# The first two of sixteen batches handled each alone in the sorting and gathering stages of a graph network

## The chip, the cores and the metric

The kernel runs on one core of a Trainium2 chip. A core has a matrix engine (PE, with its weight loads shown apart as PEld), a vector engine (DVE), a scalar engine (ACT), a general engine (POOL) and a queue engine that here only starts transfers (SP). The metric is device time in microseconds (us), the median over runs. "Faster" and "slower" are meant against the kernel before, run on the same chip.

## The reference

Sixteen batches of 1024 nodes with 64 features each and a 0/1 adjacency matrix of 1024 x 1024 (about 4 neighbours a node) go through four residual layers, each `x = x + layer(max(layernorm(x), 0), adj)`:

- layer 0: product with the adjacency plus self-loops, scaled on both sides by the root of the degree, times a 64 x 64 matrix, relu;
- layer 1: three such hops one after the other, all four stages together times a matrix, plus a bias;
- layer 2: for each node a weighted sum of three quantiles (0.25, 0.5, 0.75) of each feature over its neighbours and itself, then a two-layer perceptron. A node with more than ten neighbours first loses some of them, and the loss holds for both ends of an edge;
- layer 3: a plain adjacency product of a 64 x 64 transform, plus a bias.

```python
sv = jnp.sort(jnp.where(valid[..., None], x[:, None, :, :], big), axis=2)
pos = jnp.clip(tau * (m - 1.0), 0.0)          # m: number of valid neighbours
q = gather(floor(pos)) * (1 - frac) + gather(ceil(pos)) * frac
agg = sum(weight * q)                          # weights 0.25, 0.5, 0.25
```

## The kernel before

Layer 2 needs, for each node, the rows of its neighbours next to each other, so that a sorting network can compare them feature by feature. The kernel takes the batches two by two: eight pairs. For each pair there are two halves of work, both written in `fast` (L2044).

`first(pair)`:

- *graph0*, *graph1* (`fast_graph`, L1273), one for each batch: eight tiles of 128 adjacency rows come from memory by SP into one of four row buffers; PE transposes them, ACT writes them as fp8 into `at`, ACT and DVE count, and DVE finds the positions of the first eight neighbours (`found`).
- *lists* (`by_degree`, L1303, and `dilated`, L1396): the 2 x 1024 nodes are ordered by degree into 16 blocks (`S`), each with 64 nodes (`HP`) of one batch on the lower 64 partitions and 64 of the other on the upper. Nodes of block 0 may have more than eight neighbours: POOL fetches their full adjacency rows by an indirect transfer into `high` (L1407), and DVE reads them in `past` (L1414). The stage ends with the index lists `idx` and the quantile weights.
- *layers0*, *layers1* (`fast_to_table`, L1794): layers 0 and 1 of one batch, that is four adjacency products (`prod`), each with an ACT pass `u` behind it; then the normalised `h` is written by ACT's DMA queue into `table`, a tensor in memory with the rows of both batches.
- *rare* (`packed`, L1515): the few nodes with more than nine valid entries get their further indices packed.

`second(pair)`:

- *gather16*, *gather8*, *gather5* (`fast_quantiles`, L1601): POOL issues one indirect transfer (`gather`, L1532) for each block and neighbour number, which puts 128 rows of `table` into `slots`. `CAPS` says how many a block needs, `GROUPS` which blocks are sorted together: block 0 alone in a network of 16, blocks 1 to 6 in networks of 8, blocks 7 to 15 in networks of 5. Block 0 has nine transfers of its own, one of packed rare indices (`got`, L1537, which PE spreads with the matmuls `rare`) and one for the node itself; the others have `CAPS` plus itself. That is 86 for a pair. The last pair cuts the third group into a 5 and a 4.
- *sort16*, *sort8*, *sort5* (`compared`, L1558): DVE runs the compare-exchange networks and sums by weight into `agg`, which is split into three 16-bit parts.
- *unsort* (`unsorted`, L1711): back to node order. For each block DVE writes a 0/1 matrix `back`, and PE multiplies the three parts with it: 16 blocks x 3 parts x 2 batches x 2 halves = 192 matmuls with 64 contracted rows each.
- *out0*, *out1* (`fast_to_output`, L1870): perceptron, layer 3, result to memory.

The program calls `first(0)`, and then for each pair `first(pair + 1)` and `second(pair)`. This is not the order of execution: every operation is noted by `Plan.note` (L361), and `Plan.order` (L412) arranges all of them by a list scheduler, with a modelled duration and landing time (`cost`, L506) and a due time for each stage and pair (`WANTED`, L149, 23 stages x 8 pairs). `Plan.issue` then emits them in that order from L495, so nearly every instruction in the trace stands at L495 and is told apart by its operands. Each engine's queue is thus one fixed order; POOL's holds the `high` gathers and the row gathers of all pairs one behind the other. In `cost`, an indirect transfer takes 1.38 and lands after

```python
return 1.38, 1.7 if out.shape[-1] < N else 3.5      # L513-514; out of N or more: the high rows
```

in the scheduler's own units; these are not measured times.

Tables exist more than once and are used in turn (`self.tables[pair % len(self.tables)]`), and so are the buffers of each phase.

Of the kernel before, what the change touches and what calls it, by code (L numbers as in the profile page):

```python
# [23 lines left out]
P = 128  # L24
# [3 lines left out]
F = 64  # L28
# [12 lines left out]
CAPS = (15, 7, 6, 6, 5, 5, 5, 4, 4, 4, 3, 3, 3, 2, 2, 1)  # L41
GROUPS = ((0, 1, 16), (1, 7, 8), (7, 16, 5))
PAY = E + 3

NETS = (
# [49 lines left out]
WEIGHED = (  # L95
# [4 lines left out]
ADDED = (  # L100
# [4 lines left out]
LAST_GROUPS = (*GROUPS[:-1], (7, 12, 5), (12, 16, 4))  # L105
LAST_NETS = (
    *NETS[:-1],
# [21 lines left out]
    *WEIGHED[:-1],  # L129
# [4 lines left out]
    *ADDED[:-1],  # L134
    ((5, 0, 2, 2), (5, 0, 1, 1)),
    ((3, 0, 1, 2), (1, 1, 2, 3), (4, 0, 1, 1)),
)
FULL = 1
# [11 lines left out]
    "cells": (-238, 424, 470, 815, 927, 816, 1455, 1240),  # L150
    "const": (-127, -97, -54, -87, -26, 53, 92, 130),
    "gather16": (-320, 656, 868, 854, 1050, 1295, 1563, 1378),
    "gather4": (932, 827, 907, 1006, 1324, 1439, 1758, 1922),
    "gather5": (718, 624, 460, 714, 1049, 1015, 1225, 1795),
    "gather8": (-187, 861, 1244, 1124, 1559, 1596, 1708, 1672),
    "graph0": (121, 435, 480, 407, 973, 766, 1340, 1470),
    "graph1": (-272, 331, 531, 808, 1245, 1113, 1408, 2213),
    "layers0": (70, -98, 97, 77, 308, 585, 1093, 1356),
    "layers1": (263, 464, 588, 915, 832, 1050, 1312, 2006),
    "lists": (124, 563, 698, 686, 965, 1121, 1451, 1437),  # L160
    "out0": (-133, 489, 557, 659, 1058, 1166, 1508, 2220),
    "out1": (-24, 70, 154, 231, 695, 804, 1077, 1509),
    "rare": (340, 337, 385, 505, 923, 954, 1478, 1312),
    "sort16": (-64, 647, 651, 894, 1226, 1187, 1475, 1758),
    "sort4": (252, 1204, 1304, 1422, 1709, 1881, 2198, 1916),
    "sort5": (248, 1092, 1063, 1277, 1658, 1352, 2202, 1597),
    "sort8": (-310, -3, -266, 45, 246, 232, 788, 950),
    "strike": (267, 762, 802, 915, 1177, 1361, 1733, 2291),
    "unsort16": (348, 373, 375, 447, 889, 957, 1237, 1085),
    "unsort4": (226, 294, 346, 425, 709, 861, 1140, 920),  # L170
    "unsort5": (395, 460, 451, 701, 1158, 1004, 1359, 1044),
    "unsort8": (428, 583, 525, 959, 933, 1459, 1499, 1074),
# [132 lines left out]
class Carved:  # L305
# [6 lines left out]
    def tile(self, shape, dtype, name, tag=None):  # L312
# [21 lines left out]
        return self.made[key]  # L334

# [170 lines left out]
def cost(engine, op, out, ins, kw):  # L506
# [6 lines left out]
    if op == "indirect_dma_start":  # L513
        return 1.38, 1.7 if out.shape[-1] < N else 3.5
# [40 lines left out]
class Kernel:  # L555
    phase = ""

    def __init__(self, tc, ins, out):
        self.tc, self.nc, self.ins, self.out = tc, tc.nc, ins, out
        self.B = ins["x"].shape[0]  # L560


    def constants(self, pool, work):
# [18 lines left out]
        pair_of = self.counted(pool, work, "pair_rows", [self.B // 2], [[-FIRST, self.B // 2]], step=1)  # L582
        late = work.tile([P, self.B // 2], F32, name="late_rows")
# [35 lines left out]
        for name in ("L1_gnn_b", "L2_gnn_b2", "L3_gnn_bias"):  # L619
            t = pool.tile([P, F], F32, name=f"bias_{name}")  # L620
            nc.gpsimd.dma_start(
                out=t, in_=ins[name].rearrange("(o f) -> o f", o=1).to_broadcast([P, F])
            )
            self.bias[name] = t
# [15 lines left out]
        self.over = pool.tile([P, self.B // 2], F32, name="over")  # L640
# [18 lines left out]
    def sorted_constants(self, pool, work):  # L659
        nc = self.nc  # L660
        pairs = self.B // 2
# [42 lines left out]
        self.table_at = pool.tile([P, 1], F32, name="table_at")  # L704
        nc.gpsimd.tensor_scalar(self.table_at, late, float(N + 1), None, ALU.mult)
        pair = self.counted(work, work, "pair_of", [pairs], [[2, pairs]])
        nc.gpsimd.tensor_tensor(pair, pair, late.to_broadcast([P, pairs]), ALU.add)
        self.row_at = pool.tile([P, pairs], F32, name="row_at")
        nc.gpsimd.tensor_scalar(self.row_at, pair, float(N), None, ALU.mult)
        self.cell_at = pool.tile([P, pairs], F32, name="cell_at")  # L710
        nc.gpsimd.tensor_scalar(self.cell_at, pair, float(N * N), None, ALU.mult)
# [8 lines left out]
        self.caps = pool.tile([P, S], F32, name="caps")  # L720
        near = (NEAR, *CAPS[1:])
        for c in sorted(set(near)):
            a = near.index(c)
            nc.vector.memset(self.caps[:, a : a + near.count(c)], float(c))
# [3 lines left out]
        self.spare = pool.tile([P, 1], F32, name="spare")  # L728
        nc.gpsimd.tensor_scalar(self.spare, place, float(FIRST), None, ALU.is_ge)
# [7 lines left out]
        for n, (k, w) in enumerate(SHARED):  # L737
            nc.gpsimd.tensor_scalar(held, place, float(w), None, ALU.is_lt)
            nc.gpsimd.tensor_tensor(self.caps[:, 0:1], self.caps[:, 0:1], held, ALU.add)
# [48 lines left out]
        self.rows = [pool.tile([P, N + E], F32, name=f"row{n}") for n in range(ROWS)]  # L788
        self.high = pool.tile([P, N + E], F32, name="high")
        for r in [*self.rows, self.high]:  # L790
            nc.vector.memset(r[:, N : N + E], 1.0)
        self.slots = [
            pool.tile([P, hi - lo, n, F], F32, name=f"slots{n}") for lo, hi, n in GROUPS
# [421 lines left out]
    def redo(self):  # L1215

        nc, tc = self.nc, self.tc
        with ExitStack() as ctx:
            pool = self.pool(ctx, "redo", 1)
            self.off_diag = pool.tile([P, P], BF16, name="off_diag")  # L1220
            self.keys = pool.tile([P, N], F16, name="keys")
            self.pools(ctx, "redo", False)
            batch = pool.tile([1, self.B // 2, 2], F32, name="batch_flags")
            for i in range(2):
                flags = self.any_node(
                    pool,
                    self.ps_tr,
                    f"batches{i}",
                    self.over,
                    self.halves[:, i : i + 1],  # L1230
                    [(self.struck[:, i, n : n + 1], self.pair_rows) for n in range(2)],
                )
                nc.vector.tensor_copy(batch[:, :, i], flags)
            batch = batch.rearrange("o a b -> o (a b)")
# [68 lines left out]
    def by_degree(self, pair, zeros, founds):  # L1303
# [4 lines left out]
        pay = self.pay[pair % len(self.pay)]  # L1308
        hot = p.tile([P, 2, T, C], BF16, name="hot")
        for i in range(2):  # L1310
# [13 lines left out]
            b = 2 * pair + i  # L1324
            nc.scalar.copy(pay[:, mine, E + 2], self.mask[:, b * T : (b + 1) * T])
        w = T * C
        tb_ps = self.ps_tr.tile([w, 2, P], F32, name="tb", tag="tr")
        tb = p.tile([w, 2, P], BF16, name="tb_sb")
        for i in range(2):
# [3 lines left out]
        ps = self.ps_tr.tile([P, 2, w], F32, name="ranks", tag="tr")  # L1333
        for i in range(2):
# [3 lines left out]
        mine = p.tile([P, 2 * w], F32, name="mine")  # L1338
# [6 lines left out]
        rank = p.tile([P, 2 * T], I32, name="rank")  # L1345
        nc.vector.tensor_reduce(rank, mine.rearrange("p (s c) -> p s c", c=C), AX.X, ALU.add)
        place = p.tile([P, 2 * T], I32, name="place")
        nc.vector.tensor_scalar(place, rank, HP - 1, None, ALU.bitwise_and)
        tile_of = p.tile([P, 2 * T], I32, name="tile_of")
        nc.vector.tensor_scalar(tile_of, rank, 6, None, ALU.arith_shift_right)  # L1350
        tile_hot = p.tile([P, 2 * T, S], F16, name="tile_hot")
        nc.vector.tensor_tensor(
            tile_hot,
            self.sixteen.unsqueeze(1).to_broadcast([P, 2 * T, S]),
            tile_of.unsqueeze(2).to_broadcast([P, 2 * T, S]),
            ALU.is_equal,
        )
        there = self.p_lists.tile([P, 2 * T, HP], F16, name="there", bufs=1)
        nc.vector.tensor_tensor(
            there,  # L1360
            self.numbers[:, 0:HP].unsqueeze(1).to_broadcast([P, 2 * T, HP]),
            place.unsqueeze(2).to_broadcast([P, 2 * T, HP]),
# [3 lines left out]
        for a in range(0, 2 * T, HT):  # L1366
            shape = [P, HT, S, PAY]
# [6 lines left out]
        ps = self.ps_tr.tile([P, S, PAY], F32, name="sorted", tag="tr")  # L1374
        for t in range(T):
            for i in range(2):
                nc.tensor.matmul(
                    ps[i * HP : (i + 1) * HP].rearrange("p s c -> p (s c)"),
# [6 lines left out]
        near = self.p_lists.tile([P, S + 1, E], F32, name="near")  # L1385
        nc.scalar.copy(near[:, 0, :], ps[:, 0, 0:E])
        nc.scalar.copy(near[:, 2 : S + 1, :], ps[:, 1:S, 0:E])
        who = self.p_lists.tile([P, S + 1], F32, name="who")
        nc.scalar.copy(who[:, 0:1], ps[:, 0, E + 1 : E + 2])
        nc.scalar.copy(who[:, 1 : S + 1], ps[:, :, E + 1])  # L1390
        allowed = self.p_lists.tile([P, 1], F32, name="allowed")
        nc.scalar.copy(allowed, ps[:, 0, E + 2 : E + 3])
        nc.scalar.copy(self.degrees[pair], ps[:, :, E])
        return near, who, allowed

    def dilated(self, pair, near, who, allowed):  # L1396
# [4 lines left out]
        counts, gone = self.counts[pair], self.gone[pair]  # L1401
# [3 lines left out]
            at_row, who[:, 0:1], float(N - 1), self.row_at[:, pair : pair + 1], ALU.min, ALU.add  # L1405
# [15 lines left out]
        both = p.tile([P, 2, S + 1, E], F32, name="both")  # L1421
        own, good = both[:, 0], both[:, 1]
        nc.vector.tensor_tensor(
            own, near, who.unsqueeze(2).to_broadcast([P, S + 1, E]), ALU.is_equal
# [25 lines left out]
        for n in range(2):  # L1450
# [14 lines left out]
            base, who[:, 0:1], self.cell_at[:, pair : pair + 1], None, ALU.add  # L1465
# [6 lines left out]
        for i in range(2):  # L1472
            nc.sync.dma_start(
                out=self.cells[pair * FIRST : (pair + 1) * FIRST, i, :],
# [7 lines left out]
        idx = self.p_lists.tile([P, S + 1, E], U32, name="idx")  # L1482
        nc.vector.tensor_scalar(idx, near, float(N), self.table_at, ALU.min, ALU.add)
        near_h = self.p_lists.tile([P, 2 * E], F16, name="near_h")
        nc.vector.tensor_scalar(near_h, near16, float(N), None, ALU.min)
        self_idx = self.p_lists.tile([P, S], U32, name="self_idx")
        nc.vector.tensor_scalar(
            self_idx, who[:, 1 : S + 1], float(N - 1), self.table_at, ALU.min, ALU.add
# [222 lines left out]
    def unsorted(self, sums, hs, who):  # L1711
# [6 lines left out]
        for i in range(2):  # L1718
            self.turned(ps[i], hs[i])
# [486 lines left out]
```

## Time and profile before

| | |
|---|---|
| median of 9 runs | 1952.91 us (1937.44 to 1965.82) |
| the profiled execution's own time | 1961.34 us |
| its span in the profile | 1959.5 us |
| its mean granted PE clock | 0.737 of full speed |
| instructions | 23508 |
| row gathers by lists (`slots<-table,idx`) | 544, busy 556.2 us, 1022 ns each |
| row gathers of the nodes themselves | 124, busy 118.7 us, 957 ns each |
| matmuls `prod<-back,agg_high` | 256, busy 67.0 us |
| DVE `back` | 128, busy 61.4 us |
| first row gathers of the eight pairs at | 140, 365, 591, 813, 1033, 1249, 1462, 1680 us |

How to read it: the profile gives, for each engine, its busy time and the groups of like instructions with their number, busy time and mean duration; the idle time before a group is put down to what ended it, which is another instruction, a DMA, "issue" (nothing that the profile shows) or "remote" (another core or a queue that the profile does not know). A window cuts a stretch out of the span and gives the busy time and the number of instructions of each engine in it. PE, DVE, ACT and POOL run side by side, so busy shares don't sum to one.

### The profile page before, as it was taken

The page shows a single profiled execution, that of the slowest core. Times are in us where ns is not written, and L with a number is a line of the kernel's source. Part 1 is how long each engine was busy: PE and PEld are TensorE (multiplying, and loading weights), DVE is VectorE, ACT ScalarE, POOL GpSimd, SP SyncE. Part 2 cuts the span into 40 slices and gives each one's busy share as a digit, 9 for nine tenths or more (in the row PEclk, how much of TensorE's full clock was granted, in tenths as well). Part 3 has the DMA queues.
Part 4 walks back from the last instruction along what each step waited for, and adds up shares of the span by engine and source line. Part 5 has one row for each costly group of instructions (what it writes and reads, how often), then busy time and mean ns, then how long its engine had stood idle before and what let it go on. Part 6 is the DMA issues. An engine that isn't in the chain of part 4 may idle for free.

```text
span 1959.5 us, 23508 instructions
## 1 busy us (share of the span) xinstructions
PE 1161.4 (59%) x8497; PEld 626.9 (32%) x8497; DVE 925.9 (47%) x2408; ACT 733.2 (37%) x2024; POOL 757.6 (39%) x846
## 2 busy tenths in 40 slices
PE   3981638745697728756396729838386637411535
PEld 2551324422353315423152305514152324100312
DVE  6730617911296507824295506933296225700391
ACT  5860428601382406604282407704282222100202
POOL 8117160446207270354406470463417171574000
PEclk9985668856698758857597858867587668655767
DMA  7231222201222113212231212311221010110000
GB/s 211 89 89 27 70 65 104 60 18 43 62 87 54 53 32 99 69 25 79 54 98 31 67 36 82 100 34 44 65 84 30 8 40 6 32 27 16 11 1 13
DMA packets 93885, 108.49 MB, mean 55 GB/s; under 512 B 65120, under 2 KB 65232, under 8 KB 93760
## 3 DMA queue, kind: packets, MB, share of 16 engines
q1 hardware_dynamic: 18944, 67.12, 10.2%
q0 software_dynamic: 23744, 27.13, 7.4%
q10 hardware_dynamic: 51072, 12.66, 3.0%
q8 instruction: 68, 1.11, 0.2%
q14 instruction: 57, 0.47, 0.1%
HBM read 98.45 MB, written 8.39 MB: 55 GB/s over the span
## 4 chain that ended last, share of the span: by engine, by line
PE 37%; another core or an unknown queue 23%; DVE 15%; issue 12%; ACT 9%; DMA 1%; POOL 1%; ACTq 0%; DVEq 0%; POOLq 0%
PE prod L495 25%; PE node L495 8%; ACT u L495 5%; DVE slots L495 4%; DVE side L495 3%; ACT junk L495 2%; DVE found L495 2%; PE tr L495 1%; ACT at L495 1%; PE hidden L495 1%; DVE back L495 1%; DVE st L495 1%; PE rare L495 1%; DVE rest L495 1%
## 5 line engine op out<-in xcount | busy, mean ns | idle before, releaser
L495 POOL DMA_INDIRECT slots<-table,idx x544 | 556.2, 1022 | 245.8 <-issue 161.5
L495 PE MATMUL prod<-at,low 128*64 128x512 fp8e4 x1280 | 238.1, 405 | 57.1 <-issue 52.1
L495 PE MATMUL prod<-at,rest 128*64 128x512 fp8e4 x1280 | 240.3, 411 | 53.1 <-issue 43.5
L495 PE MATMUL prod<-at,u 128*64 128x512 fp8e4 x1280 | 237.9, 414 | 33.9 <-issue 19.9
L495 ACT ACTIVATE u<-node,d 128x64 f32<-128x64 f32 x640 | 141.3, 341 | 217.6 <-remote 162.6
L495 DVE TENSOR_SCALAR back<-numbers,who 128x1024 bf16<-128x1024 f16 x128 | 61.4, 492 | 321.6 <-remote 281.0
L495 POOL DMA_INDIRECT got<-table,rare x8 | 11.6, 1445 | 485.4 <-DMA table<-h 197.9
L495 PE MATMUL prod<-back,agg_high 64*64 64x512 bf16 x256 | 67.0, 494 | 201.3 <-issue 102.6
L495 ACT COPY rest<-prod 128x512 f32<-128x512 f32 x80 | 47.2, 590 | 302.9 <-remote 135.8
L495 DVE FIND_INDEX8 found<-ones,row 128x8 uint32<-128x1032 f32 x128 | 156.9, 1228 | 0.0
L495 PE MATMUL tr<-ident_bf,row 128*128 128x128 bf16 x1024 | 91.5, 244 | 101.1 <-ACT at L495 75.2
L495 ACT ACTIVATE junk<-row,unit 128x1024 fp8e4<-128x1024 f32 x122 | 143.5, 1177 | 16.2 <-DMA row<-in_adj_dram 14.3
L495 ACT ACTIVATE u<-x,off,by 128x64 f32<-128x64 f32 x384 | 134.6, 445 | 37.1 <-DVE off L495 23.3
L495 ACT ACTIVATE at<-tr 128x1024 fp8e4<-128x1024 bf16 x128 | 130.9, 1045 | 26.1 <-remote 17.2
L495 DVE TENSOR_TENSOR rest<-u 128x512 f32<-128x512 f32 x80 | 55.0, 688 | 165.7 <-ACT u L495 147.6
L495 POOL DMA_INDIRECT slots<-table,self_idx x124 | 118.7, 957 | 37.8 <-issue 37.2
L495 PEld LDWEIGHTS <-low 128*64 128x64 bf16 x1280 | 82.3, 115 | 147.2 <-issue 79.9
L495 PEld LDWEIGHTS <-rest 128*64 128x64 bf16 x1280 | 82.9, 116 | 140.5 <-issue 72.9
L495 PE MATMUL node<-wbd,ft_sb 128*128 128x128 f32 x512 | 101.3, 311 | 34.0 <-issue 28.3
L495 PEld LDWEIGHTS <-u 128*64 128x64 bf16 x1280 | 78.5, 116 | 119.4 <-issue 59.0
L495 PEld LDWEIGHTS <-row 128*128 128x128 bf16 x1024 | 74.6, 111 | 127.4 <-issue 107.7
L495 PEld LDWEIGHTS <-agg_high 64*64 64x64 bf16 x512 | 25.4, 125 | 251.8 <-issue 180.2
(254 smaller groups left out, 2144.3 us busy)
## 6 DMA issues: line engine op xcount, KB each, us to landing
row<-in_adj_dram SPq DMA_DIRECT2D x128, 512.0 KB
slots<-table,idx POOLq DMA_INDIRECT x544
x<-in_x_dram ACTq DMA_DIRECT2D x32, 128.0 KB
table<-h ACTq DMA_DIRECT2D x32, 128.0 KB
out_dram<-u ACTq DMA_DIRECT2D x32, 128.0 KB
slots<-table,self_idx POOLq DMA_INDIRECT x124
cells<-cell SPq DMA_DIRECT2D x16, 0.2 KB
side<-in_L_gnn_W_dram POOLq DMA_DIRECT2D x2, 64.0 KB
```

What stands on the lines that cost most here:

```text
L495: f(*[real(x) for x in s.args], **{k: real(x) for k, x in s.kw.items()})
```

## The change

The list of pairs becomes a list of nine sets: batch 0 alone, batch 1 alone, and then the seven pairs of the other fourteen. A set of one batch has 8 blocks of 128 nodes instead of 16 blocks of 2 x 64. Its `CAPS`, `GROUPS` and networks are cut to that: blocks 1 to 3 in networks of 8, blocks 4 to 7 in networks of 5, and 9 + 1 + 1 + 28 + 7 = 46 gathers a set. Its unsort has 8 blocks x 3 parts x 2 halves = 48 matmuls with 128 contracted rows. Tables of a single set hold one batch.

The assumed landing of the high rows in the scheduler's model goes from 3.5 to 8.0, and `WANTED` gets new due times for 23 stages x 9 sets. Over the whole program the order written out holds 92 row gathers where the first pair had 86, and one more `high` gather; 7786 planned PE instructions instead of 7869; and 2341 of DVE instead of 2209.

The four row buffers become slices of one tile, the slots of the last pair's extra group lie in those rows, and three bias rows are kept in a work area and read again in the part that handles batches which don't fit (`redo`).

```diff
-CAPS = (15, 7, 6, 6, 5, 5, 5, 4, 4, 4, 3, 3, 3, 2, 2, 1)
-GROUPS = ((0, 1, 16), (1, 7, 8), (7, 16, 5))
+CAPS = {
+    1: (15, 6, 5, 5, 4, 3, 3, 2),
+    2: (15, 7, 6, 6, 5, 5, 5, 4, 4, 4, 3, 3, 3, 2, 2, 1),
+}
+GROUPS = {1: ((0, 1, 16), (1, 4, 8), (4, 8, 5)), 2: ((0, 1, 16), (1, 7, 8), (7, 16, 5))}
...
+FEWER = ({1: 1}, {6: 3, 3: 1, 1: 0}, {9: 4, 8: 4, 6: 3, 3: 1})
+
+def fewer(net, tiles):
+    out = []
+    for n, wires, how, *kept in net:
+        if tiles[n]:
+            kept = [{k: (tiles.get(m, 0), a, z) for k, (m, a, z) in x.items()} for x in kept]
+            out.append((tiles[n], wires, how, *kept))
+    return tuple(out)
+
+NETS = {1: tuple(fewer(n, t) for n, t in zip(PAIR_NETS, FEWER)), 2: PAIR_NETS}
...
-    "gather16": (-320, 656, 868, 854, 1050, 1295, 1563, 1378),
+    "gather16": (-251, 395, 865, 1154, 1076, 1352, 1519, 1989, 1587),
...
     if op == "indirect_dma_start":
-        return 1.38, 1.7 if out.shape[-1] < N else 3.5
+        return 1.38, 1.7 if out.shape[-1] < N else 8.0
...
+        b = range(self.B)
+        self.sets = [b[0:1], b[1:2], *(b[n : n + 2] for n in range(2, self.B, 2))]
...
-        for s in range(S):
+        for s in range(deep):
...
-                for i in range(2):
+                for i in range(many):
                     for h in range(2):
-                        mine = slice(i * HP, (i + 1) * HP)
+                        mine = slice(i * wide, (i + 1) * wide)
...
-        for pair in pairs:
-            if pair + 1 < len(pairs):
-                first(pair + 1)
+        for g in range(len(self.sets)):
+            if g + 1 < len(self.sets):
+                first(g + 1)
             else:
                 self.strike()
-            second(pair)
+            second(g)
```

Here `many` is the number of batches in the set, `wide` is 128 divided by it, and `deep` the number of blocks, 8 or 16.

## The prediction

> **What bounds the kernel now.** I read the page first, then the waits, then windows and timelines around the first gathers. The sum is made against the profiled execution: 1961.34 us, of which the span is 1959.5. That is 8.4 us (0.4%) above the median of 1952.91 us, so what comes out as a difference is laid on the median. About 0.5% is what a measurement of this kernel can tell from no change; the nine runs alone lie between 1937.44 and 1965.82.
>
> On the page no engine is full, PE the most, and the chain that ended last goes through four engines and through "issue" and "unknown" time. The costliest group is the row gathers of POOL.
>
> ```profile
> PE 1161.4 (59%) x8497; PEld 626.9 (32%) x8497; DVE 925.9 (47%) x2408; ACT 733.2 (37%) x2024; POOL 757.6 (39%) x846
> ...
> PE 37%; another core or an unknown queue 23%; DVE 15%; issue 12%; ACT 9%; DMA 1%; POOL 1%; ACTq 0%; DVEq 0%; POOLq 0%
> ...
> L495 POOL DMA_INDIRECT slots<-table,idx x544 | 556.2, 1022 | 245.8 <-issue 161.5
> ```
>
> So I looked in the waits for what the unknown time is (waited for: us in total, times, longest):
>
> ```profile
> DVE back L495 <- remote: 281.0, 24, 56.2
> PE prod L495 <- issue: 234.8, 115, 27.9
> ACT u L495 <- remote: 204.2, 8, 41.7
> ...
> POOL got L495 <- DMA table<-h: 197.9, 3, 88.5
> ```
>
> "Remote" and "issue" name no instruction of this core. Their place shows in the table of windows (window, length, then busy us and count of PE, PEld, DVE, ACT, POOL, then the granted clock, DMA share, GB/s):
>
> ```profile
> 140.00:158.00 18.00, 12.83 (x83) 8.14 (x84) 4.09 (x7) 9.88 (x19) 13.73 (x14) 0.69 0.31 83
> 158.00:204.00 46.00, 0.48 (x5) 0.32 (x4) 1.57 (x5) 1.75 (x8) 34.77 (x37) 0.54 0.14 26
> 204.00:250.00 46.00, 35.53 (x272) 21.84 (x273) 32.62 (x79) 28.93 (x84) 0.65 (x1) 0.75 0.21 71
> 300.00:365.00 65.00, 56.33 (x500) 31.17 (x500) 56.01 (x159) 58.12 (x155) 0.00 (x0) 0.90 0.35 114
> 365.00:424.00 59.00, 30.97 (x240) 15.91 (x240) 29.64 (x60) 15.01 (x52) 46.17 (x42) 0.72 0.13 23
> ```
>
> From 140 us on POOL issues gathers back to back. PE goes on for 18 us, then executes 5 matmuls in 46 us, and is back as soon as the stream ends. Two rows of ACT's timeline in that stretch (start, length, instruction, idle before) show that this is not a wait for data of the program: nothing runs for 34.30 us, and the matmuls that `u` reads had ended by 156.8.
>
> ```profile
> 156.88 0.19 ACT L495 ACTIVATION_READ_ACCUMULATOR junk<-row,unit 128x1 f32 x1
> 191.37 1.75 ACT L495 ACTIVATE u<-node,d 128x64 f32<-128x64 f32 x8 [34.30 <-remote]
> ```
>
> The second kind is the stream of 365 to 424 us: 42 gathers at 1.40 us, and PE still at 240 matmuls, half of the dense rate of 500 in 65 us. **So gather time and PE time mostly add up** instead of lying beside each other; POOL is 39% busy and still on the path. A pair takes some 219 us: 86 gathers at 1.25 us, 107 us, and about as much dense PE work.
>
> A page of the Trainium skill speaks against this reading: "SBUF — State Buffer", section "Who interferes with whom", says that PE and ACT never wait for another engine at these ports, and DMAs contend with no engine. By it PE would work through the stream; the windows of this case say otherwise, and they decide.
>
> **The change part by part.**
>
> *a. The first table comes earlier.* POOL's first gather waits for the table:
>
> ```profile
> 140.25 1.46 POOL L495 DMA_INDIRECT got<-table,rare  x1 [63.90 <-DMA table<-h]
> 142.01 0.95 POOL L495 DMA_INDIRECT slots<-table,idx  x1 [0.30 <-issue]
> 143.26 0.94 POOL L495 DMA_INDIRECT slots<-table,idx  x1 [0.30 <-issue]
> ```
>
> It now needs both batches; afterwards batch 0 alone. ACT's timeline shows batch 0's chain, one `u` from each product to the next:
>
> ```profile
> 56.25 0.72 ACT L495 ACTIVATE u<-node,d 128x64 f32<-128x64 f32 x3
> ...
> 71.47 1.72 ACT L495 ACTIVATE u<-node,d 128x64 f32<-128x64 f32 x8
> ...
> 83.43 1.71 ACT L495 ACTIVATE u<-node,d 128x64 f32<-128x64 f32 x8
> ...
> 96.22 1.74 ACT L495 ACTIVATE u<-node,d 128x64 f32<-128x64 f32 x8 [1.03 <-PE node L495]
> ```
>
> Steps of 15.2, 12.0 and 12.8 us. The last, to 116.7, took 20.5 because batch 1's products lie between; alone I take the mean of the two before, 12.4. Then 7.8 to the last `h` (116.7 to 124.5), 2.7 from the last table DMA to the gather (137.5 to 140.2). From 56.2: 56.2 + 15.2 + 12.0 + 12.8 + 12.4 + 7.8 + 2.7 = 119, against 140: 21 us earlier. Bounds: 127 if batch 1 still lies between, 101 if PE order alone decides (508 planned PE instructions stand ahead of this gather instead of 693, and 137.5 x 508/693 = 101).
>
> *b. Batch 0's gathers.* 8 blocks of 128 need 9+1+1+28+7 = 46 gathers: 46 x 1.25 = 57.5 us, so to 177. This stream is like that of 140 to 204: PE runs for some 12 to 18 us and stops to about 182 (5 us after the end, as at 204). If PE kept going, batch 1 would not be held at all.
>
> *c. Batch 1.* About one product of it is done by 131. After 182 its chain is 15.2 + 12.0 + 12.8 + 12.4 + 7.8 + 2.7 = 63: gathers from 245. PE needs less: 950 - 508 = 442 planned instructions between the two tables, at 0.14 us (65 us / 500 matmuls x 8497 records / 7869 planned) 62, of which 10 are over. Before, POOL's second stream stood from 251 to 296.
>
> *d. Batch 1's gathers and the third table.* 46 more. If at 1.40 us with PE half alive (the row of 365) they end at 309, with some 220 of the 575 instructions that are still ahead of the third table (1525 - 950) done; the other 355 take 50: gather at **361**. If PE stops in this stream too, it ends at 303, PE is back at 308, and a chain of 63 to 72 and 9 us of queue give 371 to 388. If neither stream stops PE, about 345. Before: 365. I take 361, as the table of batches 2 and 3 is ready only because PE already has their two graphs to do meanwhile, as in the stream of 365: -4.
>
> *e. Less PE work.* The two single sets unsort with 2 x 8 x 3 x 2 = 96 matmuls of 128 rows instead of 192 of 64; 96 x 0.262 (67.0 us / 256, the `agg_high` row) = 25 us of PE. The written order agrees: after the table of batches 2 and 3, 5544 instead of 5696 planned PE instructions up to the last table, 152 x 0.14 = **-21**; behind the last table 717 instead of 677, **+6**. They count in full only in dense stretches, as 300 to 365; nothing if PE waits there anyway.
>
> *f. What is added.* Networks: a pair's take 15, 22 and 16 us; a single set's 15, 11 and 7 by their tiles, so 2 x 33 - 53 = +13; lists, 16 us a pair, are done once more on half the width: 0 to +16. Together +13 to +29 of DVE. Cover: the stretch of 158 to 250 in which DVE is busy 34 of 92 us. I cost it at nothing; without the cover, up to +29. Six more gathers, 92 for 86, and one `high` gather are in the streams of b and d.
>
> *g. The later arrival (3.5 to 8.0).* It moves only the order. `past`, which reads the high rows, starts 60 to 80 us behind its gather in pairs 1 to 6; only in pair 0 does DVE wait for it, 1.0 us. Worth 0 to -1.
>
> *h. New due times* re-order every set. No row shows their worth. The gathers of the pairs start at 365, 591, 813, 1033, 1249, 1462, 1680: periods of 226, 222, 220, 216, 213, 218. If all six were as the best, -37; as the worst, +41. I take 0, the middle, and keep these ends for the range.
>
> **Sum:** -4 - 21 + 6 = -19 in 1961: 1942, and on the median **1934 us**.
>
> **The rivals.**
>
> *Same.* The third table is late by what the stopped PE costs: 371 to 388 instead of 361, so +6 to +23 in the place of -4; with -15 of e: -9 to +8, **1944 to 1961**. For it: the row of 158 to 204 is what a first gather stream looks like here, and there would be two; a start 21 us earlier is only a stop 21 us earlier. Against it: more PE work is ready at 245 than at 158.
>
> *Slower.* Batch 0's stream freezes batch 1's chain, and everything of batches 2 and 3 queues behind batch 1 on PE. The gathers for batches 2 and 3 start at 380 to 388 (+15 to +23), and the DVE work of f, which then meets the lists and networks of the next pairs in the dense stretch (DVE 56 of 65 us in 300 to 365), has no cover: +13 to +29. With -15 of e, +13 to +37, in the middle +25: **1966 to 1990**, middle 1978. It decides if fewer than some 100 matmuls are executed between 135 and 175 us and the third table's gather is later than 380. Against it: the page's DVE is 47% busy, and DVE stands still in such streams (`back` 281 us for "remote"), so there is room.
>
> *Larger gain.* PE works through batch 0's stream, because 46 gathers are fewer than 57: third table at 345, -20 - 15 = -35, and due times on the good side: **1895 to 1918**.
>
> *The change doesn't do what it says:* the earlier table isn't used, because POOL's fixed order holds something of batch 1 ahead of batch 0's gathers (before, the `high` gather of pair 1 held the second half of the stream to 251). The order written out has batch 0's 46 in one piece, so I give it no time of its own; it would fall under "same".
>
> **Chances.** Forecast (1918 to 1943) 0.40; larger gain 0.08; same 0.17; slower 0.35. Faster by over 0.5% is thus 0.48, within 0.5% 0.17, slower 0.35. The range has to reach into the slower case: 1900 to 1980 leaves out some 0.05 below (h at its best) and 0.13 above. The forecast's own range is 1918 to 1943.
>
> **What would show it.** a: first gather of `got` at 115 to 125 us. b: a window of 135 to 175 with few matmuls. c: second stream from about 245. d: third set's gathers at about 361, half-alive PE in the stream ahead of it. e: 96 fewer `agg` matmuls, seven pairs with periods about 3 us shorter than 219. f: DVE busy about 940 to 955 us. g: `past` with its idle time as before. The forecast is wrong if the third set's gathers start later than 371, or if the periods of the seven pairs are longer than before: then it is the order (h), not the start.

## The result, and the profile after

The changed kernel is slower: 1965.5 us in the median of 20 runs, against 1948.5 us for the kernel before (62 runs, the ones shown at first among them), 17 us or 0.9% more. The ratio of 1.0119, interval 1.0097 to 1.0142, is taken from fast runs alone, which leaves out the 22 of the 62 runs of the kernel before that are over 1.5% above their fastest, and so it is on the high side; the means of all runs give 1.0089. The forecast was 1934 us, 19 below the 1952.9 of before from which it started, so the direction is wrong. Two repetitions gave 1.0094 (1.0059 to 1.0130) and 1.0070 (1.0039 to 1.0102).

The profiled execution took 1958.8 us (span 1956.9). Its page, with the lines that answer to those shown of before:

```profile
PE 1126.0 (58%) x8421; PEld 615.8 (31%) x8421; DVE 945.6 (48%) x2550; ACT 737.0 (38%) x2038; POOL 778.4 (40%) x869
...
PE 32%; another core or an unknown queue 26%; DVE 16%; issue 12%; ACT 10%; POOL 2%; DMA 1%; ACTq 0%; DVEq 0%
...
L537 POOL DMA_INDIRECT slots<-table,idx x549 | 566.2, 1031 | 252.0 <-issue 162.9
```

In these two profiles PE is 35 us less busy, and DVE 20 us more. The unsort accounts for most of the first: its six groups of matmuls take 381 us instead of 413. The share of the chain that is put down to something unknown has grown. The waits (us in total, times, longest):

```profile
DVE back L537 <- remote: 258.5, 23, 33.8
...
ACT rest L537 <- remote: 213.3, 12, 58.5
...
PE prod L537 <- issue: 199.1, 84, 21.7
```

They are of the same kind as before. Where the time went is read from POOL's timeline, at the first gathers of batch 0, of batch 1 and of batches 2 and 3 (start, length, instruction, idle before):

```profile
117.56 0.97 POOL L537 DMA_INDIRECT got<-table,rare  x1 [35.51 <-DVE pay L537]
...
245.47 1.09 POOL L537 DMA_INDIRECT got<-table,rare  x1 [70.66 <-DVE slots L537]
...
374.85 1.61 POOL L537 DMA_INDIRECT slots<-table,idx  x1 [67.94 <-DMA table<-h]
```

The forecast had 119, 245 and 361 for these, and the kernel before had the third at 365. The windows between them (length, busy us and count of PE, PEld, DVE, ACT, POOL, granted clock, DMA share, GB/s):

```profile
129.00:175.00 46.00, 3.39 (x18) 2.79 (x17) 0.00 (x0) 2.25 (x6) 34.84 (x37) 0.55 0.16 26
175.00:245.00 70.00, 56.54 (x441) 31.40 (x443) 51.96 (x143) 38.97 (x131) 0.00 (x0) 0.88 0.07 20
245.00:307.00 62.00, 24.96 (x147) 13.53 (x141) 10.32 (x33) 8.82 (x25) 45.00 (x47) 0.67 0.22 49
307.00:375.00 68.00, 57.06 (x471) 34.52 (x473) 52.05 (x158) 48.90 (x135) 0.15 (x1) 0.90 0.24 79
```

The first and third row are the two gather streams. In the first, PE stands still, and not it alone: DVE executes nothing and ACT 6 instructions. In the third PE executes 147 matmuls, where the forecast had counted on half the dense rate, which 240 in 59 us had shown for another stream.

To see whether the loss is there or later, the program is cut at the first gathers of the sets. "Third" is the one for batches 2 and 3; the periods run from one pair's first gather to the next pair's. Single profiles of both kernels, all with spans of 1935 to 1978 us:

| | third | six periods | sum | last gathers to end |
|---|---|---|---|---|
| before | 365 | 226 221 220 216 213 218 | 1315 | 280 |
| before, again | 365 | 218 221 218 215 211 205 | 1288 | 281 |
| after | 375 | 214 201 221 236 211 212 | 1296 | 286 |
| after, again | 374 | 212 197 223 237 212 209 | 1290 | 285 |
| after, third time | 376 | 219 211 224 238 215 208 | 1317 | 286 |

Up to the third gathers 10 us are lost, at the end 5, and the six periods are level: 1301.5 and 1301. They are level by two things that cancel: the first two are 25 us shorter (418 for 443), and the fourth is 21 us longer (237 for 215.5).

### The profile page after: what moved, and what is told of

Its sections match the earlier page's. It is cut to its first block, busy times and chain, and to the rows that moved or that the text cites. A ratio compares the mean times of both kernels' runs of the same rounds, so it can differ in the third digit from the quotient of the medians.

```text
span 1956.9 us, 23586 instructions
## 1 busy us (share of the span) xinstructions
PE 1126.0 (58%) x8421; PEld 615.8 (31%) x8421; DVE 945.6 (48%) x2550; ACT 737.0 (38%) x2038; POOL 778.4 (40%) x869
## 4 chain that ended last, share of the span: by engine, by line
PE 32%; another core or an unknown queue 26%; DVE 16%; issue 12%; ACT 10%; POOL 2%; DMA 1%; ACTq 0%; DVEq 0%
PE prod L537 22%; PE node L537 6%; ACT u L537 5%; DVE slots L537 4%; DVE side L537 4%; DVE found L537 2%; ACT junk L537 1%; ACT at L537 1%; PE rare L537 1%; DVE back L537 1%; PE tr L537 1%; DVE st L537 1%; PE hidden L537 1%; DMA row<-in_adj_dram 1%
## 5 line engine op out<-in xcount | busy, mean ns | idle before, releaser
L537 POOL DMA_INDIRECT slots<-table,idx x549 | 566.2, 1031 | 252.0 <-issue 162.9
L537 POOL DMA_INDIRECT got<-table,rare x9 | 17.4, 1930 | 550.4 <-DVE slots L537 209.3
L537 PE MATMUL prod<-back,agg_high 64*64 64x512 bf16 (+1 forms) x256 | 65.6, 487 | 241.3 <-issue 99.0
L537 DVE TENSOR_TENSOR x<-x,u 128x512 f32<-128x512 f32 x32 | 22.1, 691 | 222.7 <-ACT u L537 213.5
L537 DVE TENSOR_TENSOR side<-slots 128x256 f32<-128x256 f32 (+6 forms) x160 | 89.9, 601 | 72.9 <-ACT slots L537 71.8
L537 PE MATMUL node<-wbd,rest 128*128 128x128 f32 x256 | 43.9, 318 | 133.3 <-issue 74.5
L537 PE MATMUL node<-wbd,ft_sb 128*128 128x128 f32 x512 | 94.7, 300 | 39.3 <-ACT ft_sb L537 29.0
```

What stands on the lines that cost most here:

```text
L537: f(*[real(x) for x in s.args], **{k: real(x) for k, x in s.kw.items()})
```

## The experiments

**Theories.** *Start*: the change loses before the third gathers, because batch 0's stream holds batch 1's chain and batch 1's stream holds the next table. *Rest*, or *order*: it loses in the seven pairs, by the new due times or the 8.0. *Hidden*: early gathers lie beside PE work.

**1. Both kernels again.** No edit.

> The kernel before, unchanged, for a second profile and for the spread of one kernel against itself: ratio 1.00 within 0.5%. The first profile was of a long execution (1961 against a median of 1948 to 1953). Start theory (the change loses its time before the gathers of batches 2 and 3): those gathers stand clearly below 365 here, at 350 to 358, and the periods of the later pairs sum to about 1315 again. Order theory (it loses it in the seven pairs, by the new due times and the 8.0): the gathers stand at 365 again and the six periods sum to 1300 or less.

> The changed kernel, unchanged, for a second profile: ratio 1.009 to 1.014. Both theories: first gathers at 118, batch 1's at 245, as in the first profile, since the chains before them are fixed. Start theory: third set's gathers at 375 or later, six periods about 1295. Order theory: third set's gathers at 365 to 375 and the six periods over 1305.

Measured: 1.0002 (0.9964 to 1.0039) and 1.0094 (1.0059 to 1.0130). The third gathers of before stood at 365 again and the periods summed to 1288, as the order theory had it and not the start theory. In the changed kernel they stood at 374 and the periods summed to 1290, near the start theory and below the order theory's 1305. Neither theory had both; up to the third gathers 10 us are lost, and that is not all.

**2. The assumed landing alone**, in the kernel before and, backwards, in the changed one:

```diff
-        return 1.38, 1.7 if out.shape[-1] < N else 3.5
+        return 1.38, 1.7 if out.shape[-1] < N else 8.0
```

> The kernel before with only the assumed landing of the high rows at 8.0 instead of 3.5; this reorders instructions and changes no work. Start theory: no difference from before, ratio 0.997 to 1.004. Order theory with the 8.0 as its cause: 1.008 or more.

> The changed kernel with the landing back at 3.5: nine sets and new due times stay. Start theory: like the changed kernel, 1.009 to 1.014. Order theory with the 8.0 as its cause: 1.004 or less.

Measured: 1.0001 (0.9967 to 1.0035) and 1.0108 (1.0044 to 1.0171). The 8.0 is worth nothing that can be measured in either structure. Where the time goes does change with it, as the marks of these two profiles show:

| | third | six periods | sum | last gathers to end |
|---|---|---|---|---|
| before, with 8.0 | 383 | 212 212 221 221 211 200 | 1277 | 282 |
| after, with 3.5 | 372 | 226 218 215 214 219 230 | 1322 | 278 |

In the kernel before the third gathers moved to 383 and it still cost nothing; so that mark alone doesn't decide the end, and a count of the cost has to go by whole times. In the changed kernel the short first periods and the long fourth one are gone, and the loss is not.

**3. Without the early gathers**, by which the cost of the streams is measured by itself. The same edit with `pair == 0` in the kernel before:

```diff
+                    self.plan.steps[-1].skip = many == 1
...
         for s in self.order():
+            if s.skip:
+                continue
```

> The changed kernel without 90 of the 92 gathers of batches 0 and 1 (the two packed ones stay), every other instruction in the same order; the output for these two batches is therefore not the reference's. Start theory (the two early streams are where the change loses): this kernel and the next one are equal within 0.4%, both some 75 to 90 us below the kernels that they come from. Rest theory (it loses in the seven pairs and at the end): this one stays 12 to 25 us above the next. Hidden-transfer theory (early gathers lie beside PE work): both only 0 to 20 us below their originals.

> The kernel before without 85 of the 86 gathers of its first pair (the packed one stays), all else in the same order; the output of batches 0 and 1 is not the reference's. If streams stop PE it gains 109 us of stream less the 26 us of PE that ran in them, about 80: 0.955 to 0.962 of before. If gathers were hidden: 0.99 to 1.00.

Measured: 0.9998 (0.9967 to 1.0029) and 1.0042 (1.0011 to 1.0073), but of a kernel before that took **1224.4 us**. These runs fell on a chip on which the whole program takes 37% less time, and the gathers cost nothing there. They could not tell the theories apart on the first kind of chip, so they were made again beside the changed kernel, and came on a chip of the first kind:

> The changed kernel, unchanged, as the mark for the other three on one chip. The last four runs fell on a chip on which the kernel before takes 1224 us instead of 1950 and PE runs through the gather streams. Start theory on a chip of the first kind: 1.009 to 1.014 of before again. On a chip of the second kind the early streams hide beside PE work, and what is left of the change is an earlier table, 25 us less PE work and 13 to 29 us more DVE work: 0.985 to 1.005.

> The changed kernel without 90 of the 92 gathers of batches 0 and 1 (their output is not the reference's), all else in the same order. On a chip of the first kind, start theory: within 0.4% of the next kernel, and 75 to 90 us below the changed kernel. Rest theory: 12 to 25 us above the next kernel. On a chip of the second kind: 1.00 of before, as in the run before.

> The kernel before without 85 of the 86 gathers of its first pair (batches 0 and 1 are not the reference's), all else in the same order. On a chip of the first kind: 0.955 to 0.962 of before, 109 us of stream less 26 us of PE work in them. On a chip of the second kind: 1.00, as in the run before.

Measured: before 1953.7, changed 1970.3 (ratio 1.0070, 1.0039 to 1.0102), without early gathers 1863.7 (0.9528, 0.9483 to 0.9574) and 1866.5 (0.9539, 0.9487 to 0.9592). **The 90 early gathers cost the changed kernel 107 us, the 85 of the kernel before 87 us** (by the ratios 106 and 90). That is over the 75 to 90 expected for the changed kernel and a little over the 80 for the kernel before. Without them the two kernels are equal within their intervals: the start theory's expectation, and against the rest theory, which had 12 to 25 us between them. It is just outside: from the two intervals I estimate that up to some 11 us could still lie there. POOL's timeline of the changed kernel without early gathers shows what each stream holds, and a row of the kernel before without them where its third gathers start:

```profile
190.88 1.10 POOL L539 DMA_INDIRECT got<-table,rare  x1 [73.32 <-DVE slots L539]
...
269.48 1.29 POOL L539 DMA_INDIRECT slots<-table,idx  x1 [68.28 <-DVE found L539]
```

```profile
264.74 0.94 POOL L497 DMA_INDIRECT slots<-table,idx  x1 [70.27 <-DVE pos L497]
```

Batch 1's gathers could start at 191 instead of 245, so batch 0's stream of 57 us delays them by 55. The third could start at 269 instead of 375; of these 105 us the second stream, of 62, makes up 51. In the kernel before, without its early gathers, the third starts at 265 instead of 365: streams of 109 us cost 100. So the earlier first table brings the third one nothing even without streams (269 against 265).

Up to the third gathers the streams thus cost 105 us and 100, and in the whole time 107 and 87 to 90: behind that mark the kernel before gets 10 to 13 us back and the changed one nothing. In which periods it does is not seen in single profiles: without early gathers the six periods sum to 1302 in the changed kernel and 1315 in the kernel before, with them to 1290 to 1317 and 1288 to 1315.

**4. One stream left out at a time.** `g == 0` and `g == 1` in the place of `many == 1`.

> The changed kernel without 45 of the 46 gathers of batch 0 alone (its output is not the reference's), all else in the same order. On the two chips of the first kind the 90 early gathers cost the changed kernel 107 us (1970 to 1864) and 85 cost the kernel before 87 us. If batch 0's stream is paid in full because batch 1's chain stands behind it: 50 to 58 us below the changed kernel, 0.975 to 0.982 of before. If batch 0's stream is half hidden and batch 1's is the dear one (the failed step d): 40 to 48 below, 0.983 to 0.988. On a chip of the second kind: 0.99 to 1.00.

> The same without 45 of the 46 gathers of batch 1 alone instead. If PE stands in batch 1's stream and what it still does there is of no use: 55 to 62 us below the changed kernel, 0.974 to 0.980 of before. If PE is half alive in it, as the prediction had it: 25 to 35 below, 0.990 to 0.996. On a chip of the second kind: 0.99 to 1.00.

> The changed kernel, unchanged, as the mark on this chip. First kind of chip: 1.007 to 1.014. Second kind (the kernel before at 1224 us): 0.985 to 1.005, since there the gathers lie beside PE work.

> The changed kernel without 45 of the 46 gathers of batch 0 alone (its output is not the reference's), all else in the same order; the run before fell on a chip of the second kind and gave 0.994. On a chip of the first kind: if batch 0's stream is paid in full because batch 1's chain stands behind it, 0.975 to 0.982 of before; if half of it is hidden, 0.983 to 0.988.

> The same without 45 of the 46 gathers of batch 1 alone instead. On a chip of the first kind: if PE stands in batch 1's stream and what it still does there is of no use, 0.974 to 0.980 of before; if PE is half alive in it, as the prediction had it, 0.990 to 0.996. On a chip of the second kind: 0.995, as before.

Both times the chip was of the second kind: 0.9937 (0.9903 to 0.9971) and 0.9945 (0.9909 to 0.9980) without batch 0's, 0.9950 (0.9919 to 0.9981) and 0.9977 (0.9953 to 1.0001) without batch 1's. The changed kernel itself is at **0.9973** (0.9947 to 1.0000) of before on such a chip, 1222.6 us against 1225.3: no loss. Beside it each stream is worth 0.4% or less there, which the intervals don't tell from nothing. On a chip of the first kind these two were not run; what each stream costs there rests on the timelines of experiment 3.

**5. What in a stream stops PE: POOL being busy, or the gathers?** Each of the 90 is replaced:

```diff
             if s.skip:
+                for _ in range(8):
+                    self.nc.gpsimd.memset(real(s.kw["out"]), 0.0)
                 continue
```

> The changed kernel with each of the same 90 gathers replaced by eight POOL memsets of 64 elements on the same slots, about 1 us together; batches 0 and 1 come out wrong. Gathers-stop-PE theory: PE runs through these stretches at its dense rate (over 60 matmuls in 10 us) and the time is within 15 us of the kernel without the 90 gathers. Any-busy-POOL theory: PE stands in them as before, and the time is within 15 us of the changed kernel.

> The changed kernel with the 90 gathers replaced by eight POOL memsets each, about 1 us together (batches 0 and 1 are not the reference's). On a chip of the first kind: gathers-stop-PE theory within 15 us of the kernel without the 90 gathers; any-busy-POOL theory within 15 us of the changed kernel. On a chip of the second kind: 1.00 of before.

The first fell on the second kind of chip, 1.0033. The second, on the first kind: 1867.6 us (0.9551, 0.9498 to 0.9603), 4 us from the kernel without the gathers. The window of 129 to 175 us, in which the changed kernel executes 18 matmuls; first with memsets in their place, then with nothing:

```profile
129.00:175.00 46.00, 40.80 (x326) 23.32 (x325) 39.26 (x102) 28.14 (x94) 34.22 (x237) 0.96 0.07 24
```

```profile
129.00:175.00 46.00, 40.94 (x327) 24.28 (x326) 40.90 (x107) 28.10 (x93) 0.00 (x0) 0.96 0.08 24
```

A POOL that is busy for 34 of 46 us with memsets stops nothing; 37 gathers do. And the same window, and that of the second stream, of the changed kernel with all its gathers, on the second kind of chip:

```profile
129.00:175.00 46.00, 42.32 (x327) 23.41 (x328) 41.38 (x107) 27.00 (x88) 36.25 (x33) 0.93 0.20 46
...
245.00:307.00 62.00, 54.47 (x443) 31.03 (x439) 56.58 (x173) 47.41 (x136) 35.33 (x33) 0.92 0.36 95
```

327 matmuls, to the piece what PE does with no gathers at all. The same program, the same data, the same order: on one chip the gathers lie beside PE work, on another they stop it.

**6. The due times.** The changed kernel with those of before, batches 0 and 1 with the first pair's:

```diff
+WANTED = {k: (v[0], *v) for k, v in WANTED.items()}
```

> The changed kernel with the due times of before: batches 0 and 1 both take those of the first pair, the other seven theirs. The landing stays at 8.0. Order theory (the new due times are the loss, as in the blocked gather of 14.4 us at 1012): 0.997 to 1.004 of before. Structure theory (nine sets lose in any order): 1.008 to 1.02.

Measured on the second kind of chip: 1.0229 (1.0187 to 1.0272), over both expectations, where the changed kernel with its own times has 0.9973 (on another chip of this kind). The order alone is worth 2.6% there, and the new due times are a gain on such a chip. It doesn't speak for the order theory on the first kind of chip, where it wasn't run.

**7. Single batches at the end instead.**

```diff
-        self.sets = [b[0:1], b[1:2], *(b[n : n + 2] for n in range(2, self.B, 2))]
+        self.sets = [*(b[n : n + 2] for n in range(0, self.B - 2, 2)), b[self.B - 2 : self.B - 1], b[self.B - 1 :]]
```

> The changed kernel with the two single batches at the end (14 and 15) instead of at the start, the last group no longer split, and due times set for that order with less search than those of the changed kernel. All kernels have some 280 us from the first gather of the last set to the end (188 on a chip of the second kind), with PE idle for 93. On a chip of the first kind, if the last stream of 112 us and the networks behind it are halved: 30 to 60 us below before, 0.97 to 0.985. If the second single's gathers must wait for the first one's networks, because they share the slots: 0.995 to 1.02.

Second kind of chip: 1258.2 us, 1.0263 (1.0216 to 1.0311). With experiment 6 in mind, this may be its due times and not the place of the singles; it settles nothing but that this version is no gain. No version that beats both kernels on the first kind of chip came out of these runs.

## Why the prediction was wrong

Two terms of the sum failed: d, the start, stood at -4 and measured +10, because PE does little in batch 1's stream (147 matmuls in 62 us, of which 11 us are hidden) where d had it half alive; and the six periods, e's -21 with h's 0, measured 0. The first is shown. The second is open as to its cause.

- **a, b and c held.** First gathers at 118 (119 forecast), batch 0's stream to 175 (177), PE stopped in it, 18 matmuls from 129 us on (12 to 18 us of work and then none), batch 1's gathers at 245 (245).
- **d failed, by 14 us.** It gave batch 1's stream the half-alive PE of the stream at 365 and had the third gathers at 361; they came at 374 to 376, as in the alternative that it had worked out and not taken. The forecast meant that 27 of the stream's 64 us would be hidden (116 us from batch 1's gathers to the third, against 79 without a stream in experiment 3); of the 62 us measured, 11 were. The row at 365 is the kindest of the early streams of the kernel before. The first one had 5 matmuls in 46 us in the same table, and the second, in a row that was not shown there, 15 in 37 us:

```profile
263.00:300.00 37.00, 5.39 (x15) 3.21 (x15) 0.00 (x0) 1.68 (x3) 24.69 (x27) 0.50 0.19 39
```

With one row for and two against, the alternative was the one to take. Its lower end of 371 leaves out the 9 us of queue (380 with them), and the 57 gathers that "larger gain" names for the first stream are 51 in the trace; neither changes the choice.
- **e had its size right and did not arrive.** The unsort matmuls take 32 us less (25 forecast), and the end is 5 us longer (6). The first two periods are 25 us shorter (21 forecast), and the fourth takes 21 us back. That those 25 us are e's isn't shown: with the landing back at 3.5 the changed kernel has the same saving and 445 us in these two periods, and the kernel before with 8.0 has no saving and 424 (experiment 2).
- **h**, priced at 0 with wide bounds, can't be told from e by these runs. What stands out in the fourth period of the changed kernel is on POOL's timeline at its start:

```profile
1010.92 0.95 POOL L537 DMA_INDIRECT got<-table,rare  x1 [81.11 <-DVE slots L537]
1012.17 14.36 POOL L537 DMA_INDIRECT slots<-table,idx  x1 [0.30 <-DVE found L537]
1026.84 2.30 POOL L537 DMA_INDIRECT slots<-table,idx  x1 [0.30 <-issue]
```

One gather lasts 14.36 us instead of 0.95. DVE's timeline beside it is a closed row of instructions with two operands each, most of them from networks of the pair before:

```profile
1012.05 0.21 DVE L537 TENSOR_TENSOR slots<-slots,weights 128x64 f32<-128x64 f32 x1
1012.17 1.89 DVE L537 TENSOR_TENSOR side<-slots 128x576 f32<-128x576 f32 x3
1013.97 0.69 DVE L537 TENSOR_TENSOR rest<-u 128x512 f32<-128x512 f32 x1
1014.58 0.55 DVE L537 TENSOR_TENSOR slots<-slots 128x384 f32<-128x384 f32 x1
...
1024.41 1.30 DVE L537 TENSOR_TENSOR side<-slots 128x512 f32<-128x512 f32 x2
1025.62 0.49 DVE L537 TENSOR_SCALAR back<-numbers,who 128x1024 bf16<-128x1024 f16 x1
1026.01 0.36 DVE L537 TENSOR_TENSOR slots<-slots 128x192 f32<-128x192 f32 x1
1026.28 2.03 DVE L537 TENSOR_TENSOR slots<-side,weights 128x576 f32<-128x576 f32 x3
```

The gather ends at 1026.53, 0.9 us after the first instruction of another kind, `back`, has begun; DVE itself goes on without a gap. The long gather stands there in all three profiles (14.36, 14.38, 11.08 us). The longest in the two profiles of the kernel before lasts 5.6 us. The Trainium skill, "SBUF — State Buffer", section "Who interferes with whom", says that a DVE instruction with two inputs from that memory contends with a POOL instruction that reads it. The trace fits that, and shows that a row of them can hold one gather for 14 us.

But this gather is not what makes the kernel slower. It stands with 14.37 us in the changed kernel on the second kind of chip, which loses nothing there (0.9973), and with 11.21 us in the changed kernel without early gathers, which is level with the kernel before. With the landing back at 3.5 no row gather lasts over 4.2 us, the fourth period is 214 us, and the loss is the same (1.0108). And the kernel before with 8.0 has gathers of 10.56, 7.78 and 7.24 us and is at 1.0001 of before:

```profile
1475.89 10.56 POOL L495 DMA_INDIRECT slots<-table,idx  x1 [0.30 <-issue]
```

- **f**: 20 us more DVE were measured, inside the 13 to 29. Without the early streams the two kernels are equal (experiment 3), with e, f and h all in it, so there too nothing of the 15 us that e was to bring is seen; whether f or h eats it or it never was worth that much was not measured. **g** was right: nothing.
- **The rivals.** "Slower" had the mechanism, batch 1's chain frozen by batch 0's stream, and its 13 to 37 us hold the 17 measured. That is luck in part: its start was to cost 15 to 23 us and cost 10, its 15 us of saved PE work did not arrive, and its DVE work without cover did not show in the first periods, which were shorter. Its decision point was half met: 18 matmuls in the stream (fewer than 100), but the third gathers at 375, not over 380. It was given 0.35 and deserved more: the forecast took the whole PE gain as certain and the dead stream as an exception, though it had itself found that gather time and PE time mostly add up. "Larger gain", that PE works through batch 0's stream, is what the second kind of chip does; even there the gain is 0.3%.

The sum, by the table of the result: +10 to the third gathers, 0 in the periods (-25, +21, the rest small), +5 at the end, so 15 us in the profiles, where the forecast had -19; of these 34 us, 14 are d's and 21 the periods'. The medians give 17, the three ratios 14 to 23.

## What to carry to other kernels

Splitting a first batch to start a shared stage earlier pays only if what follows can run beside that stage; read one window in the middle of a stream, count the matmuls in it, and where they stop, price the stream nearly in full every time it occurs (here 57 us cost 55, and 62 cost 51). Work that was saved must be followed to the end of the program: here the unsort takes PE 32 us less, and the whole time shows none of it. One long wait in a timeline is not yet a cause: the gather of 14 us also stands in runs that lose nothing, and the loss also in a run without it. And a change by a new written order is two changes: leave the early streams out of both kernels, and the rest can be compared by itself.

## What the runs showed of the hardware that was not expected

The kernel before takes 1950 us on two of the chips that the runs came on and 1225 us on two others, with the same instructions. On the first kind, PE executes nothing or one instruction in 1.40 us while POOL's gathers follow each other at 1.25 us. In the stream of batch 0 it is 18 matmuls in 46 us at a granted clock of 0.55. The slow pace stands in a later stream of the kernel before, where a matmul starts every 2.80 us and a weight load halfway between (1149.34, 1152.14):

```profile
1150.74 0.58 PE L495 MATMUL prod<-at,low 128*64 128x512 fp8e4 x1 [2.21 <-issue]
1153.54 0.58 PE L495 MATMUL prod<-at,low 128*64 128x512 fp8e4 x1 [2.22 <-issue]
```

On the second kind PE executes 327 matmuls in the window of batch 0's stream, at a clock of 0.93. The rule that was weighed in the prediction, that PE and ACT never wait for another engine (the Trainium skill, "SBUF — State Buffer", section "Who interferes with whom"), fits what the second kind shows and not the first. POOL memsets in the gathers' place don't stop PE on the first kind, so it is the gathers; which part of a gather does it, and why on some chips only, these runs leave open. A low granted clock goes with the standstill; whether it is its consequence is not shown.
